# An attention kernel's row norms: channel sums by way of HBM, the root from ScalarE's logarithm and exponential, value transposes two tiles at a time

## The chip, the cores and the metric

The kernel runs on one core of one Trainium2 chip. The metric is device time in microseconds, from the first to the last instruction of the program. Before the change it is 3788.41 us, the median of three runs (3782.36 to 3791.38). All data are float32.

## The reference

The input is x, 48 channels of 256 x 256. Layer 0 is x + attention(groupnorm(x)), and layer 1 is x + window mixing(groupnorm(x)). The change lies in layer 0:

```python
qkv = jnp.einsum('bchw,oc->bohw', x, w_qkv)
qkv = dwconv3x3(qkv, w_dw)
q, k, v = jnp.split(qkv, 3, axis=1)
...
q = _l2norm(q)          # over the channels of a head's token
k = _l2norm(k)
attn = jnp.einsum('bhcn,bhcm->bhnm', q, k) * temperature
attn = jax.nn.softmax(attn, axis=-1)
out = jnp.einsum('bhcn,bhnm->bhcm', v, attn)
```

Between the split and the norm, heads() unfolds 4 x 4 patches: a token is one patch, and a head's token has 6 channels x 16 pixels = 96 entries. There are 8 heads and 4096 tokens inside the image (border tokens are zeros, and enter the softmax's sum as a constant). The norm of a token is the root of the sum of 96 squares: over 16 pixels, and over 6 channels. Queries are also scaled by the temperature, and values aren't scaled at all.

## The kernel before, in words

Everything that the change touches happens in the attention stage, from about 300 to 3320 us. Its outer loop runs over the 8 heads (h), and its inner loop over 16 steps (g) of G = 2 blocks of 128 tokens each. The order of instructions is written out by hand there (tc.manual_schedule): every engine runs its own instructions in the order of the program's text, and waits where its operands or buffers aren't ready.

In step g:

- scores (L536) multiplies a block of 128 queries with all 4096 keys in four PSUM tiles of 1024 columns ("big", three buffers of two banks), six matmuls a tile (logits, L341). ScalarE takes the exponential of each tile (L545) and so frees the tile. Scores of block 2g+1 and of block 2g+2 are made in step g, one step ahead of use.
- normalised (L554) divides the values' tile by the sums of the exponentials on VectorE (L558 to L564): vn.
- weigh (L567) runs for k = 0 to 3. It multiplies the exponentials of both blocks with vn in 64 matmuls (L574) into one "big" tile, and VectorE adds this tile to oacc (L585), which frees it.

So a step takes twelve "big" tiles, in the order weigh 0 to 3 and then eight tiles of logits for the next step; "big" has three buffers, so a tile may be begun when the tile three before it has been read.

Beside this, step g prepares the next head (h+1), one row of patches at a time. The class Depthwise is such a row: 126 partitions, which are 7 bands of the image x 18 channels (6 each of queries, keys and values), and 64 patches. Row r passes through three steps: g = r (n: first), g = r+1 (d: taps, square, reduce, norm, root, scale) and g = r+2 (p: high, low, store). There are ten rows, so d is there for g = 1 to 10. In detail:

- load (SyncE) brings the padded pixels; first (L217, ScalarE) is the first of the nine taps of the 3 x 3 convolution, and tap (L236, VectorE) each of the eight others, 1024 elements a partition.
- square (L247, ScalarE) and reduce (L251, VectorE) give the sum over 16 pixels, ss, 126 x 64.
- norm (L255) adds the six channels on TensorE: a product with "same", a 126 x 126 matrix of ones and zeros, into the PSUM tile pn.
- root (L257) makes the inverse root on VectorE: a first value from integer arithmetic on the bits (L268), three Newton steps of three operations each (L273 to L275), and the affine y * nmul + nadd (L276), which puts the temperature in and leaves values alone.
- scale (L281, VectorE) multiplies the row by it: o, in the order of patches.
- high (L290, ScalarE) rounds o to the format of the fast matmul (oh), low (L294, GpSimd) takes the difference (ol), and store (L299) writes o, oh and ol to the DRAM tile qkv of the head, from GpSimd's queue. Values are read from part 2 (o), queries and keys from parts 0 and 1.

Most row tiles have one buffer (cv pool); sq and ol share one ("t4"), so the next row's square waits until ol has been written out.

load_value (L519) reads 512 tokens of a head's values into vt (two buffers), and turn (L525) transposes such a tile on TensorE into the PSUM tile pst (pool "one", two buffers; pn and the output's transposes live there too); ScalarE copies it out (L530). For the next head, two value tiles are loaded in each of the steps g = 11 to 14, and turned in the same step, one after weigh k = 0 and one after k = 2. Tile m has tokens 512m to 512m + 511; row r of band j holds the tokens 576j + 64r to 576j + 64r + 63.

In head 0, each weigh is also followed by a Strip: the 1 x 1 convolution of two pixel rows for the heads 2 to 7, a product into a "big" tile (L185) which ScalarE reads (L188). With it a step has 16 "big" tiles.

The first head's own rows (depthwise_first) are made before the attention stage; they use norm and root with ScalarE's square root, and the change leaves them as they are.

Of the kernel before, what the change touches and what calls it, by code (L numbers as in the profile page):

```python
# [8 lines left out]
F32 = mybir.dt.float32  # L9
F32R = mybir.dt.float32r  # L10
AF = mybir.ActivationFunctionType
ALU = mybir.AluOpType
# [17 lines left out]
CR = 9  # L30
# [14 lines left out]
def conv_preact_kernel(  # L45
# [28 lines left out]
    t1 = [dram.tile([(h1 - h0) * HC, TR, W + 2], F32, name=f"t1_{h0}") for h0, h1 in GROUPS]  # L74
    qkv = [dram.tile([3, CH, HC * KK, CN + PX], F32, name=f"qkv{h}") for h in range(NH)]

    os_ = dram.tile([NT // TP, C * KK, TP], F32, name="os_")
    x1s = dram.tile([C, H, W], F32, name="x1s")

# [119 lines left out]
    class Depthwise:  # L199
# [53 lines left out]
        def norm(self):  # L253
            self.pn = one.tile([NP1, PX], F32, name="pn", tag="one")
            nc.tensor.matmul(self.pn, lhsT=same, rhs=self.ss, start=True, stop=True)  # L255

        def root(self, on_scalar=False):  # L257
            n = self.pool.tile([NP1, PX], F32, name="n", bufs=2)
            nc.vector.tensor_scalar_max(n, self.pn, 1e-24)
            y = self.pool.tile([NP1, PX], F32, name="y", bufs=2)  # L260
            if on_scalar:
                nc.scalar.activation(n, n, AF.Sqrt)
                nc.vector.reciprocal(y, n)
                nc.vector.tensor_scalar(y, y, nmul[:, self.h : self.h + 1], nadd, ALU.mult, ALU.add)
                self.y = y
                return

            nc.vector.tensor_scalar(  # L268
                y.bitcast(mybir.dt.int32), n.bitcast(mybir.dt.int32), -0.5, 1597463007.0, ALU.mult, ALU.add
            )  # L270
            z = self.pool.tile([NP1, PX], F32, name="z", bufs=self.bufs)
            for _ in range(3):
# [230 lines left out]
    with tc.tile_pool(name="ahead", bufs=2) as ah, tc.tile_pool(name="ae", bufs=3) as ae, tc.tile_pool(  # L503
# [110 lines left out]
        with tc.manual_schedule():  # L614
            load_query(0, 1)
            block = scores(0, 0)
            for h in range(NH):
                more = h + 1 < NH
                rows = {r: Depthwise(h + 1, r) for r in range(CR + 1)} if more else {}
                for g in range(NG):  # L620
# [17 lines left out]
                        load_query(h, g + 2)  # L638
                    elif more:
                        load_query(h + 1, g + 2 - NG)  # L640
                    if p:
                        p.store((2,))
                    if d:
                        for t in range(1, 4):
                            d.tap(t)
# [9 lines left out]

                    if g == 0 and rows:
                        rows[0].load()
                    if p:
                        p.high()
                    if d:  # L660
                        d.square()
                    if n:
                        n.first()
                    for k in range(NK):
                        s = (h * NG + g) * NK + k
                        weigh(h, g, blocks, k)
                        if k == 0 and d:
                            d.reduce()
                        if k == 0 and p:
                            p.low(nc.gpsimd)  # L670
                            p.store((0, 1))
                        for w in strips[s]:
                            w.run(big.tile([128, 2, 512], F32, name="big"))
                        for w in strips[s + 2]:
                            w.load()
                        for w in strips[s - 1] if s else []:
                            w.store()
                        if k == 2 and d:
                            d.norm()
                            d.root()  # L680
                        if k == 2 and g + 1 in rows:
                            rows[g + 1].load()
                        if k == 3 and d:
                            d.scale()
                        if h == 0 and 0 < g <= 6 and k == 0:
                            turn(0, g + 1)
                        if more and CR + 2 <= g < CR + 6 and k in (0, 2):
                            turn(h + 1, (g - CR - 2) * 2 + k // 2)

                        if g == 0 and h > 0 and k == 0:  # L690
                            for m in range(6, 8):
# [248 lines left out]
```

## Time and profile before

| | busy us | share of the span |
|---|---|---|
| TensorE, matmul (PE) | 3511.2 | 93% |
| TensorE, weight load (PEld) | 2913.1 | 77% |
| VectorE (DVE) | 2201.6 | 58% |
| ScalarE (ACT) | 1719.0 | 45% |
| GpSimd (POOL) | 599.8 | 16% |

The span of the profiled run is 3787.3 us. A busy share is a mean over stages: the attention stage has ten steps of a head with depthwise work and six without, and VectorE's load is very different in the two. Rows of the profile name a line (L574), an engine, an operation and the tiles as out<-in. A group's row ends with its busy time and the mean of one instruction in ns, and then the idle time of its engine just before it, with what ended that. In a timeline, the columns are the start in us, the time taken, the engine and the instruction, how many were merged, and in brackets the idle time before. Queues are written as SPq, ACTq and POOLq.

Some rows that the change touches, each as count and mean of one:

| instruction | count | mean ns |
|---|---|---|
| L255 PE matmul into pn | 160 records (two for each of 80 products) | 299 |
| L251 DVE reduce 1024 to 64 | 80 | 1217 |
| L273, L274, L275 DVE, 64 elements | 210 each | 225, 226, 225 |
| L281 DVE scale, 1024 elements | 75 | 1992 |
| L290 ACT high | 80 | 1038 |
| L294 POOL low | 80 | 2368 |
| L299 POOL, issue of a store | 70 to 80 for each of three | 1231 to 1339 |
| L528 PE transposes of values | 256 records | 259 |
| L530 ACT copy of the transposed tile | 64 | 478 |
| ACT table loads | 3 | 1283 |

### The profile page before, as it was taken

The page shows a single profiled execution, that of the slowest core. Times are in us where ns is not written, and L with a number is a line of the kernel's source. Part 1 is how long each engine was busy: PE and PEld are TensorE (multiplying, and loading weights), DVE is VectorE, ACT ScalarE, POOL GpSimd, SP SyncE. Part 2 cuts the span into 40 slices and gives each one's busy share as a digit, 9 for nine tenths or more (in the row PEclk, how much of TensorE's full clock was granted, in tenths as well). Part 3 has the DMA queues.
Part 4 walks back from the last instruction along what each step waited for, and adds up shares of the span by engine and source line. Part 5 has one row for each costly group of instructions (what it writes and reads, how often), then busy time and mean ns, then how long its engine had stood idle before and what let it go on. Part 6 is the DMA issues. An engine that isn't in the chain of part 4 may idle for free.

```text
span 3787.3 us, 99981 instructions
## 1 busy us (share of the span) xinstructions
PE 3511.2 (93%) x44216; PEld 2913.1 (77%) x44216; DVE 2201.6 (58%) x3520; ACT 1719.0 (45%) x2668; POOL 599.8 (16%) x595
## 2 busy tenths in 40 slices
PE   1867999999999999999999999999999999955998
PEld 0225777788888888888888888888888889812776
DVE  5572775169727962895299439934992222266564
ACT  0224665555545554555455445545554444300222
POOL 0030121012301220121122112211220000000011
PEclk9888999999999999999999999999999999966999
DMA  6575666534533542354244424432443100299784
GB/s 138 168 177 153 185 192 172 167 110 118 116 83 99 125 110 75 104 127 106 81 109 117 100 83 117 116 98 76 123 114 93 41 21 19 44 243 188 122 145 90
DMA packets 307459, 441.64 MB, mean 117 GB/s; under 512 B 98298, under 2 KB 232778, under 8 KB 302792
## 3 DMA queue, kind: packets, MB, share of 16 engines
q1 hardware_dynamic: 253590, 270.32, 27.5%
q0 software_dynamic: 48320, 156.61, 18.5%
q10 hardware_dynamic: 5106, 8.21, 1.0%
q8 instruction: 351, 5.75, 0.6%
q14 instruction: 92, 0.75, 0.1%
HBM read 234.76 MB, written 199.95 MB: 115 GB/s over the span
## 4 chain that ended last, share of the span: by engine, by line
PE 82%; DMA 6%; issue 2%; DVE 1%; SPq 1%; ACT 0%; POOL 0%; ACTq 0%; POOLq 0%
PE big L341 36%; PE big L574 35%; PE pb L838 4%; PE pa L816 2%; PE pc L855 2%; PE big L185 1%; DMA pad<-t 1%; DMA x1s<-pxt 1%; PE pt L591 1%; PE pst L528 1%; DMA pxt<-in_x_dram 1%; DMA pot<-os__70 1%; DMA t<-ot 1%; PE pn L255 1%; DMA qkv<-ol 0%
## 5 line engine op out<-in xcount | busy, mean ns | idle before, releaser
L545 ACT ACTIVATE e<-big,nmx 128x1024 f32<-128x1024 f32 x1024 | 1144.3, 1118 | 842.1 <-PE big L341 631.7
L341 PE MATMUL big<-kt,qt 128*128 128x512 f32 x6144 | 1438.5, 393 | 43.9 <-DMA qt<-qkv 29.9
L574 PEld LDWEIGHTS big<-vn,e 128*64 128x64 f32 x32768 | 1367.6, 137 | 86.1 <-ACT e L545 45.1
L574 PE MATMUL big<-vn,e 128*64 128x96 f32 x32768 | 1425.4, 248 | 7.5 <-ACT ot L188 4.1
L341 PEld LDWEIGHTS big<-kt,qt 128*128 128x128 f32 x6144 | 1145.4, 188 | 306.5 <-issue 44.6
L585 DVE TENSOR_TENSOR oacc<-big,oacc 128x768 f32<-128x768 f32 x480 | 458.2, 955 | 706.2 <-PE big L574 706.2
L236 DVE SCALAR_TENSOR_TENSOR acc<-pad,dwt,acc 126x1024 f32<-126x1024 f32 x600 | 777.2, 1296 | 33.6 <-ACT acc L217 17.2
L294 POOL TENSOR_TENSOR ol<-o,oh 126x1024 fp32r<-126x1024 f32 x80 | 189.4, 2368 | 942.2 <-DVE ss L251 804.7
L558 DVE TENSOR_REDUCE zt<-zs 128x1 f32<-128x4 f32 x256 | 39.0, 152 | 361.3 <-ACT e L545 361.3
L545 ACT ACTIVATION_READ_ACCUMULATOR e<-big,nmx 128x1 f32 x1024 | 196.0, 191 | 0.0
L823 DVE TENSOR_TENSOR lzt<-pa,cbias 128x864 f32<-128x864 f32 (+1 forms) x88 | 137.0, 1627 | 99.7 <-PE pa L816 99.7
L845 ACT COPY lyt<-pb 128x512 f32<-128x512 f32 x144 | 84.5, 586 | 215.7 <-PE pb L838 215.7
L299 POOL DMA_DIRECT2D qkv<-o x70 | 86.1, 1231 | 511.0 <-DVE zu L560 243.6
L595 POOL DMA_DIRECT2D os__70<-oo x128 | 65.1, 515 | 594.0 <-ACT oo L593 593.6
L247 ACT ACTIVATE sq<-acc 126x1024 f32<-126x1024 f32 x75 | 79.3, 1058 | 167.8 <-issue 112.2
L281 DVE TENSOR_TENSOR o<-acc,y 126x1024 f32<-126x1024 f32 x75 | 149.4, 1992 | 0.1
L838 PEld LDWEIGHTS pb<-wsb,lzt 128*64 128x64 f32 x2304 | 126.3, 138 | 29.2 <-issue 21.2
L838 PE MATMUL pb<-wsb,lzt 128*64 128x128 f32 x2304 | 142.7, 280 | 2.5 <-issue 2.4
L721 PE MATMUL pps<-pot,wp 96*96 96x512 f32 x128 | 77.9, 776 | 68.3 <-DMA pot<-os__70 68.3
L188 ACT ACTIVATE ot<-big,bias 108x1024 f32<-108x1024 f32 x64 | 71.1, 1112 | 153.9 <-PE big L185 72.0
L217 ACT ACTIVATE acc<-pad,dwt 126x1024 f32<-126x1024 f32 x75 | 85.3, 1137 | 73.3 <-DMA pad<-t 73.3
L721 PEld LDWEIGHTS pps<-pot,wp 96*96 96x96 f32 x128 | 26.6, 215 | 119.1 <-issue 118.6
(115 smaller groups left out, 1888.4 us busy)
## 6 DMA issues: line engine op xcount, KB each, us to landing
pad<-t SPq DMA_DIRECT2D x80, 761.9 KB
qkv<-ol POOLq DMA_DIRECT2D x80, 504.0 KB, 8.9
qkv<-o POOLq DMA_DIRECT2D x70, 504.0 KB, 6.9
qkv<-oh POOLq DMA_DIRECT2D x70, 504.0 KB, 7.4
t<-ot SPq DMA_DIRECT2D x128, 217.7 KB
qt<-qkv SPq DMA_DIRECT2D x176, 96.0 KB
xs<-in_x_dram SPq DMA_DIRECT2D x128, 96.0 KB
os__70<-oo POOLq DMA_DIRECT2D x128, 96.0 KB, 2.2
```

The lines of the kernel that those rows point to most:

```text
L217: nc.scalar.mul(self.acc, self.pad[:, 0:KS, 0:W], dwt[:, self.h, 0:1])
L236: nc.vector.scalar_tensor_tensor(self.acc, self.pad[:, dy : dy + KS, dx : dx + W], dwt[:, self.h, tap : tap + 1], self.acc, ALU.mult, ALU.add,
L281: nc.vector.tensor_tensor(self.o.rearrange("p (a b) x -> p a b x", a=KS), self.acc.rearrange("p a (x b) -> p a b x", b=KS), self.y.rearran ...
L294: eng.tensor_sub(self.ol, self.o, self.oh.bitcast(F32))
L299: eng.dma_start(out=qkv[self.h][i].rearrange("j (c k) n -> (j c) k n", k=KK)[:, :, px], in_=self.o if i == 2 else (self.ol if i else self. ...
L341: nc.tensor.matmul(ps[:, i, :], lhsT=qt[:, r, q0 : q0 + 128], rhs=kts[2 * j + i][:, r // 2, :], start=(r == 0), stop=(r == 2),)
L545: nc.scalar.activation(e[:, j * 1024 : (j + 1) * 1024], ps.rearrange("p a b -> p (a b)"), AF.Exp, bias=nmx[:, b : b + 1], accum_out=zs[:, ...
L574: nc.tensor.matmul(ps[p : p + 64, j // 4, j % 4 * HD : (j % 4 + 1) * HD], lhsT=e[:, mb * 128 + p : mb * 128 + p + 64], rhs=vn, start=(i == 0),
L585: nc.vector.tensor_add(oaccs[h, k], ps[:, :, : 4 * HD], oaccs[h, k])
L721: nc.tensor.matmul(ps[:, i : i + 2, :], lhsT=wp, rhs=ot[:, ki * KS + i : ki * KS + i + 2, :], start=True, stop=True,)
L823: nc.vector.tensor_tensor(zv[:, :, y0 : y0 + n, :], pa[:, :, : n * T3 * C].rearrange("p s (y k) -> p s y k", y=n), cbias.rearrange("p (u v ...
L838: nc.tensor.matmul(pb[s * WS : (s + 1) * WS, i, :], lhsT=zts[u][:, t * C + c + i, :], rhs=wsb[:, t, :], start=True, stop=True,)
```

## The change

The sum over the six channels leaves TensorE. Instead, gather writes ss (32 KB) to a DRAM tile on SyncE's queue, and reads it back so that each of the 126 partitions gets the six rows of its group, sg. One step later guess adds the six on VectorE, bounds the sum from below, and takes ScalarE's logarithm and then the exponential of minus one half of it as a first value of the inverse root. mend refines this with one Newton step on VectorE and applies the affine. For this, root, scale, high, low and all three stores of a row move to step g = r+2: guess stands after weigh k = 0, the rest after k = 1. first of the newest row moves behind them. The turns of the next head's values both stand after weigh k = 0. root itself stays for the branch that isn't taken here and for depthwise_first.

The aim is to free TensorE of the small products and of changes between kinds of matrices, and VectorE of two of three Newton steps.

```diff
+    ssd = [dram.tile([NP1, PX], F32, name=f"ssd{i}") for i in range(2)]
...
+        def gather(self):
+            to = ssd[self.r % 2]
+            nc.sync.dma_start(out=to, in_=self.ss)
+            self.sg = self.pool.tile([NP1, 6, PX], F32, name="sg")
+            nc.sync.dma_start(
+                out=self.sg,
+                in_=to.rearrange("(g u c) n -> g u (c n)", u=1, c=6).to_broadcast([NP1 // 6, 6, 6 * PX]),
+            )
+
+        def guess(self):
+            self.n = n = self.pool.tile([NP1, PX], F32, name="n", bufs=1)
+            nc.vector.tensor_reduce(n, self.sg.rearrange("p c n -> p n c"), AX.X, ALU.add)
+            nc.vector.tensor_scalar_max(n, n, 1e-24)
+            self.y = self.pool.tile([NP1, PX], F32, name="y", bufs=1)
+            nc.scalar.activation(self.y, n, AF.Ln)
+            nc.scalar.activation(self.y, self.y, AF.Exp, scale=-0.5)
+
+        def mend(self):
+            z = self.pool.tile([NP1, PX], F32, name="z", bufs=1)
+            nc.vector.tensor_mul(z, self.y, self.y)
+            nc.vector.scalar_tensor_tensor(z, z, -0.5, self.n, ALU.mult, ALU.mult)
+            nc.vector.scalar_tensor_tensor(self.y, z, 1.5, self.y, ALU.add, ALU.mult)
+            nc.vector.tensor_scalar(self.y, self.y, nmul[:, self.h : self.h + 1], nadd, ALU.mult, ALU.add)
...
-                    if p:
-                        p.store((2,))
...
-                    if p:
-                        p.high()
                     if d:
                         d.square()
-                    if n:
-                        n.first()
                     for k in range(NK):
                         s = (h * NG + g) * NK + k
                         weigh(h, g, blocks, k)
+                        if k == 0 and p:
+                            p.guess()
                         if k == 0 and d:
                             d.reduce()
-                        if k == 0 and p:
+                            d.gather()
+                        if k == 1 and p:
+                            p.mend()
+                            p.scale()
+                            p.high()
                             p.low(nc.gpsimd)
-                            p.store((0, 1))
+                            p.store()
+                        if k == 1 and n:
+                            n.first()
...
-                        if k == 2 and d:
-                            d.norm()
-                            d.root()
...
-                        if k == 3 and d:
-                            d.scale()
...
-                        if more and CR + 2 <= g < CR + 6 and k in (0, 2):
-                            turn(h + 1, (g - CR - 2) * 2 + k // 2)
+                        if more and CR + 2 <= g < CR + 6 and k == 0:
+                            for m in range(2):
+                                turn(h + 1, (g - CR - 2) * 2 + m)
```

More of the change, by code (lines that the diff above doesn't have):

```diff
@@ L255, in norm @@
             nc.tensor.matmul(self.pn, lhsT=same, rhs=self.ss, start=True, stop=True)
+        def gather(self):
[19 more added lines that the diff above has]
+            nc.vector.tensor_scalar(self.y, self.y, nmul[:, self.h : self.h + 1], nadd, ALU.mult, ALU.add)
         def root(self, on_scalar=False):
-            n = self.pool.tile([NP1, PX], F32, name="n", bufs=2)
+            n = self.pool.tile([NP1, PX], F32, name="n", bufs=min(self.bufs, 2))
             nc.vector.tensor_scalar_max(n, self.pn, 1e-24)
-            y = self.pool.tile([NP1, PX], F32, name="y", bufs=2)
+            y = self.pool.tile([NP1, PX], F32, name="y", bufs=min(self.bufs, 2))
             if on_scalar:
```

## The prediction

> **What bounds the kernel now.** I read the chain of work first, then busy times by stretch, then the timeline of one repeated piece, engine by engine.
>
> ```profile
> PE 82%; DMA 6%; issue 2%; DVE 1%; SPq 1%; ACT 0%; POOL 0%; ACTq 0%; POOLq 0%
> PE big L341 36%; PE big L574 35%; PE pb L838 4%; PE pa L816 2%; PE pc L855 2%; PE big L185 1%; DMA pad<-t 1%; DMA x1s<-pxt 1%; PE pt L591 1%; PE pst L528 1%; DMA pxt<-in_x_dram 1%; DMA pot<-os__70 1%; DMA t<-ot 1%; PE pn L255 1%; DMA qkv<-ol 0%
> ```
>
> TensorE's two attention products are 71% of the chain; pn (L255), which the change removes, is on it with 1%. Busy time by stretch (columns: PE, PEld, DVE, ACT, POOL):
>
> ```profile
> 1623.10:1645.40 22.30, 22.30 (x307) 19.85 (x306) 20.74 (x35) 12.69 (x19) 6.02 (x4) 1.00 0.49 120
> 3100.00:3121.80 21.80, 21.80 (x310) 19.51 (x307) 5.24 (x12) 9.65 (x16) 0.00 (x0) 1.00 0.07 20
> 385.60:412.90 27.30, 27.30 (x328) 21.36 (x327) 21.07 (x35) 17.40 (x24) 6.06 (x4) 1.00 0.72 196
> ```
>
> I call a window the time from the first weight load of weigh(k=0) to that of the next g; there are 16 in each head. The rows are a window with depthwise work (head 3), one without (head 7) and one of head 0, where strips run too. PE fills all three; but VectorE has only 1.6 us to spare in the first, so its order may decide who waits. PEld of the first window:
>
> ```profile
> 1623.10 7.95 PEld L574 LDWEIGHTS big<-vn,e 128*64 128x64 f32 x192 [0.35 <-ACT e L545]
> 1631.17 0.29 PEld L255 LDWEIGHTS pn<-ss,same 126*126 126x126 f32 x2
> 1631.53 2.67 PEld L574 LDWEIGHTS big<-vn,e 128*64 128x64 f32 x64
> 1634.32 10.75 PEld L341 LDWEIGHTS big<-kt,qt 128*128 128x128 f32 x48
> 1645.42 0.69 PEld L574 LDWEIGHTS big<-vn,e 128*64 128x64 f32 x16 [0.35 <-ACT e L545]
> ```
>
> The period is 1645.42 - 1623.10 = 22.32 us; without depthwise work it is 3120.14 - 3098.32 = 21.82 in the same view. The difference, 0.50, is pn, 1631.17 to 1631.53, and the changes of weights around it (rather 0.52 over many windows). So PE waits for nobody here, and what goes from PE comes off the time, if nothing new makes it wait.
>
> **What the Trainium skill says.** *ScalarE: Activation LUTs*, section "What ACT_TABLE_LOAD costs": a load takes 1283 ns, with a drain of about 1380 ns 2.66 us per switch. The trace has the 1283; the activation after it starts 1.3 us after the load's start, so no drain follows the load. But ScalarE had been idle, so a drain between busy activations isn't shown:
>
> ```profile
> L534 ACT ACT_TABLE_LOAD x1: 1283/1283/1283, 274.6 to 274.6; - x1
> L534 ACT ACTIVATE e<-nmx x1: 416/416/416, 275.9 to 275.9; 128x256 f32<-128x256 f32 x1
> ```
>
> The same page, "Table sets: the hidden batching unit", knows a set that holds both ln and exp. The changed program's list of ScalarE instructions doesn't use it so: a load stands ahead of each Ln and of each Exp of guess, 140 in 70 rows. *DMA: Bandwidth & Descriptors*, "Anatomy of one DMA — SWDGE (gpsimd) path", puts a transfer's fixed cost at about 2.0 us; the trace agrees, with 2.2 us for the 96 KB of os_.
>
> **The change, part by part.** Three buffers of "big" set the rule: a product may start when the one three before it has been read. In heads 1 to 6 the order is w0 to w3 (weigh), s0 to s7 (logits), so s1 needs w2 read by VectorE (L585).
>
> *1. pn goes.* 60 windows (10 in each of heads 1 to 6) x 0.52 = -31 us, if the period falls to 21.81.
>
> *2. The root moves across three engines.* VectorE loses 12 small operations: 1632.16 to 1635.30, 3.1 us. It gains a reduction of 384 (estimate 0.55: 1024 take 1.22 at L251, plus a fixed part), a maximum (0.2), one Newton step and the affine (3 x 0.26 + 0.32 = 1.1): about 1.9. The relief of 1.2 us is worth nothing by itself, but pulls the taps forward.
>
> ScalarE gains Ln and Exp (0.25 each, as L262) and two loads of 1.28. They lie in the weigh half, where it has room: 12.7 of 22.3 busy. Yet in order: Ln waits for VectorE's maximum, mend on VectorE for Exp, oh (high) for scale, and behind oh are first and the next exps.
>
> VectorE's view of the same window, for the chain:
>
> ```profile
> 1628.76 1.22 DVE L251 TENSOR_REDUCE ss<-sq 126x64 f32<-126x1024 f32 x1 [0.31 <-ACT sq L247]
> 1635.21 0.95 DVE L585 TENSOR_TENSOR oacc<-big,oacc 128x768 f32<-128x768 f32 x1
> 1636.08 1.99 DVE L281 TENSOR_TENSOR o<-acc,y 126x1024 f32<-126x1024 f32 x1
> 1642.58 0.15 DVE L558 TENSOR_REDUCE zt<-zs 128x1 f32<-128x4 f32 x1
> ```
>
> The taps now end 4.49 after the window's start, since zt at 1642.58 is held up by scale and three taps. With scale gone to the middle, zt waits only for the fourth exp (it ends 17.6 into the shorter window): zt 17.7, taps from 18.5, five of 1.31, end 25.05; that is 3.25 in the next. From there: sq to 4.4 (1.06); load 5.7; Ln 5.9; load 7.2; Exp 7.5 (all of VectorE's inputs are ready before: its maximum at 4.8); mend 8.65; scale 10.65; the reading of w2 11.5. PE wants s1 at 10.7 + 1.34 = 12.04. Slack 0.4 us: no wait if a load costs 1.28 to 1.5. With two drains of 1.38 the wait is 2.76 - 0.4 = 2.4 us in every such window. I take the trace's 1.28, and 0.15 us a window for what the slack doesn't cover, since sq also waits for the landing of ol (they share "t4"): ol would be issued at 15.2 and land 24.1, 2.3 into the next window, against 3.3; its slowest landings would miss that. 9 x 6 = 54 windows: +8 us (0 to 25).
>
> *3. Gather.* The 32 KB out and back on SyncE takes two transfers of some 2.2 us; ss is there at 6, sg by 11, needed 15 us later. The pad loads queue behind it and aren't needed before the next window. Nothing, in heads 1 to 6.
>
> *4. Two turns together.* Each block of transposes costs 0.60 now (in a window 11 the weigh loads stop at 1759.73 and go on at 1760.33). Side by side one change of weights is saved: 0.2 (0 to 0.35) x 28 = -6 us. PSUM "one" has a buffer for each.
>
> *5. The stores move later.* The o part left at 15.4 of the window before; now all three leave after low. DMAs now (KB, us to landing):
>
> ```profile
> qkv<-ol POOLq DMA_DIRECT2D x80, 504.0 KB, 8.9
> qkv<-o POOLq DMA_DIRECT2D x70, 504.0 KB, 6.9
> qkv<-oh POOLq DMA_DIRECT2D x70, 504.0 KB, 7.4
> os__70<-oo POOLq DMA_DIRECT2D x128, 96.0 KB, 2.2
> ```
>
> GpSimd: oh there at 11.7, low 2.37 to 14.1, issue of oh to 15.3, ol to 16.5, o from 16.5. It lands 6.9 us later at best, 23.4; queued behind two others (oh and ol land 2.6 us apart now, 7.4 and 1.13 + 8.9 after oh's issue) at 26.7. Who reads row 8? The second value tile: its tokens 512 to 575 are row 8, and the changed program makes that load, issued for g = 11, wait for exactly this store; before, it had landed almost a window earlier. So the load starts 1.6 to 4.9 into window 11, takes 0.8 of issue and 2.2 to 3.1 (192 KB of kt by GpSimd land in 3.1), and is there at 4.6 to 8.8. The second turn, now at k = 0, would run at 3.2; it was at k = 2 and is in PE's queue ahead of w1. PE waits 1.4 to 5.6, say 3.6, in six heads: +22 us.
>
> *6. Head 0.* Here a strip's product follows each weigh, and ScalarE must empty it. ScalarE's window of before:
>
> ```profile
> 386.82 1.04 ACT L290 CAST oh<-o 126x1024 fp32r<-126x1024 f32 x1
> 388.88 1.06 ACT L247 ACTIVATE sq<-acc 126x1024 f32<-126x1024 f32 x1 [1.02 <-DVE acc L236]
> 389.85 1.13 ACT L217 ACTIVATE acc<-pad,dwt 126x1024 f32<-126x1024 f32 x1
> 390.89 1.10 ACT L188 ACTIVATE ot<-big,bias 108x1024 f32<-108x1024 f32 x1
> 393.95 1.11 ACT L188 ACTIVATE ot<-big,bias 108x1024 f32<-108x1024 f32 x1 [1.59 <-issue]
> ```
>
> The second ot ends at 9.45, and w3 needs its buffer. In the changed order it stands behind oh and first, and oh behind scale. w1 ends at 7.0, so its reading ends at 8.2, mend 9.25, scale 11.25, oh 12.35, first 13.4, second ot 14.4. w3 can start at 14.5; it started at 397.95, or 12.34. So +2.1 us in windows 2 to 10, pn's removal included: 9 x 2.1 = +19, and +1 for window 11, with one row still to scale. (The first ot, after Exp, ends at 8.5 and holds w2 up by 0.4, which this wait swallows.) Together +20 (5 to 35: the strips' input loads also queue behind gather).
>
> *Sum:* -31 + 8 - 6 + 22 + 20 = +13 us: 3788 + 13 = 3801.
>
> **The rivals.**
> *A, faster.* The store and its reader overlap better, and head 0's strips find room. For it: PE is the bound, and 0.52 a window is sure to go. Against: the order of ScalarE's queue in head 0, and that the load names the store. -31 - 6 + 8 + 5 = -24: 3764.
> *B, ScalarE's switches become the bound.* The full 2.66. For it: the page; against: the L534 line. 54 x 2.4 + 9 x 2.76 = +155 beside +5 of the rest (the 8 are in it): 3948.
> *C, they cancel.* Smaller waits at row 8 (1.4 x 6 = 8) and head 0 (15) with all else: -31 + 8 - 6 + 8 + 15 = -6, so 3782.
>
> **How the numbers follow.** My forecast 0.46, A 0.22, B 0.12, C 0.20. Slower is the forecast and B, 0.58; same is C. The range must hold 8 in 10: downward from A's upper half, 3768; upward by +25 for part 2 and the upper ends of 5 and 6 in part, 3852. About half of A and B lie outside.
>
> **What would show it.** L255 only 10 rows, 20 records; periods of 21.8 to 22.0 in windows 2 to 10 of heads 1 to 6 (24.2 for B); 140 more loads of 1283 ns, with Ln right behind; PE waiting for a DMA of vt at L528 in six windows; PE waiting for ot (L188) before w3 in head 0, period near 29.4. Wrong it would be if windows of heads 1 to 6 stay above 22.3, or window 11 shows no wait for vt.

## The result, and the profile after

The changed kernel takes 3870.95 us (median of 6 runs, 3862.63 to 3880.75) against 3782.45 for the kernel before (6 runs, 3776.57 to 3791.38). The ratio is 1.0246, with a 95% interval of 1.023 to 1.0262: it is slower, as forecast, but by 88 us where 13 were forecast, and above the 3852 at which the forecast's range ends. The profiled spans are 3878.9 and 3787.3 us. The chain of work that ended last, first by engine and then by line:

```profile
PE 47%; DVE 22%; DMA 12%; ACT 5%; issue 4%; POOL 1%; SPq 1%; ACTq 0%; DVEq 0%; POOLq 0%
PE big L369 19%; PE big L602 18%; DVE acc L237 12%; PE pb L864 4%; DVE o L309 3%; DMA qkv<-ol 3%; DMA pxt<-in_x_dram 2%; DVE oacc L613 2%; DVE zu L588 2%; PE pa L842 2%; DMA qkv<-o 2%; ACT L274 2%; PE pc L881 2%; ACT sq L248 2%; DMA vt<-qkv 1%
```

The two attention products fell from 71% of the chain to 37%; taps, scale and zu on VectorE, and the stores of ol and o, took their place. VectorE's busy share is 58% before and after, but its work now stands in the chain that others wait for. (Lines have moved: weigh L574 is L602, logits L341 is L369, oacc L585 is L613, zu L560 is L588, low L294 is L322.)

With a window as the prediction defines it, the two profiled runs differ as follows (us, 91.6 in all):

| windows | before | after | difference |
|---|---|---|---|
| head 0, all 16 | 458.46 | 492.83 | +34.37 |
| heads 1 to 6, g = 1 | 133.96 | 130.88 | -3.08 |
| g = 2 to 10 (54 windows) | 1205.64 | 1225.53 | +19.89 |
| g = 11 (6) | 139.61 | 182.65 | +43.04 |
| g = 12 to 14 (18) | 415.80 | 410.04 | -5.76 |
| the rest (g = 0 and 15, head 7, start, end) | | | +3.1 |

Now the same views as in the prediction. Busy time by stretch (PE, PEld, DVE, ACT, POOL, then the granted clock, the DMA share and GB/s): a window with depthwise work, and the stretch behind a wait in window 11.

```profile
1679.60:1702.30 22.70, 22.14 (x307) 19.48 (x306) 21.59 (x29) 15.46 (x23) 6.09 (x4) 1.00 0.53 132
...
1828.90:1835.80 6.90, 6.90 (x133) 6.83 (x134) 2.34 (x6) 0.48 (x1) 0.00 (x0) 0.79 0.39 99
```

TensorE no longer fills the first: 22.14 of 22.70. Its weight loads in that window (head 3, g = 5):

```profile
1679.59 10.59 PEld L602 LDWEIGHTS big<-vn,e 128*64 128x64 f32 x256 [0.35 <-ACT e L573]
1690.30 1.23 PEld L369 LDWEIGHTS big<-kt,qt 128*128 128x128 f32 x6
1692.51 9.40 PEld L369 LDWEIGHTS big<-kt,qt 128*128 128x128 f32 x42 [0.98 <-DVE oacc L613]
```

pn is gone from between the weigh loads, and a wait of 0.98 us for oacc stands after the first logits tile: it is s1 waiting for the reading of w2. VectorE there:

```profile
1678.84 5.25 DVE L237 SCALAR_TENSOR_TENSOR acc<-pad,dwt,acc 126x1024 f32<-126x1024 f32 x4
...
1688.40 0.23 DVE L280 TENSOR_TENSOR z<-y 126x64 f32<-126x64 f32 x1 [0.46 <-ACT y L275]
...
1689.59 2.01 DVE L309 TENSOR_TENSOR o<-acc,y 126x1024 f32<-126x1024 f32 x1
1691.51 1.81 DVE L613 TENSOR_TENSOR oacc<-big,oacc 128x768 f32<-128x768 f32 x2
1693.24 0.15 DVE L586 TENSOR_REDUCE zt<-zs 128x1 f32<-128x4 f32 x1
1693.42 1.76 DVE L588 SCALAR_TENSOR_TENSOR zu<-e,zt 128x1 f32<-128x1 f32 x1
...
1695.41 0.96 DVE L592 TENSOR_SCALAR vn<-vT,rz 128x96 f32<-128x96 f32 x1
1695.60 3.92 DVE L237 SCALAR_TENSOR_TENSOR acc<-pad,dwt,acc 126x1024 f32<-126x1024 f32 x3
...
1699.62 0.16 DVE L588 SCALAR_TENSOR_TENSOR zu<-e,zt 128x1 f32<-128x1 f32 x1
```

The zu of one block took 1.76 us, that of the next 0.16, on operands of the same shape. The long one ended at 1695.18. GpSimd there:

```profile
1692.76 2.40 POOL L322 TENSOR_TENSOR ol<-o,oh 126x1024 fp32r<-126x1024 f32 x1 [16.59 <-ACT oh L318]
1695.11 1.23 POOL L327 DMA_DIRECT2D qkv<-oh  x1
1696.25 1.35 POOL L327 DMA_DIRECT2D qkv<-ol  x1
1697.37 1.47 POOL L327 DMA_DIRECT2D qkv<-o  x1
```

low ended at 1695.16. In all, 60 of the 256 zu take 1.75 to 1.78 us, one in each window of heads 1 to 6 in which low runs. vn, 0.27 for the next block, took 0.96 while the first issue ran, but the taps behind it still began 0.19 after it, as they do behind a short one. Before, low ran from 6.96 to 9.32 of a window, beside the readings of weigh tiles in PSUM, and zu was short (low, then VectorE):

```profile
1630.06 2.36 POOL L294 TENSOR_TENSOR ol<-o,oh 126x1024 fp32r<-126x1024 f32 x1 [12.68 <-DVE ss L251]
```

```profile
1631.29 0.96 DVE L585 TENSOR_TENSOR oacc<-big,oacc 128x768 f32<-128x768 f32 x1 [0.45 <-PE big L574]
...
1638.16 0.16 DVE L560 SCALAR_TENSOR_TENSOR zu<-e,zt 128x1 f32<-128x1 f32 x1
```

ScalarE of the changed kernel in the window of g = 5:

```profile
1684.18 1.06 ACT L248 ACTIVATE sq<-acc 126x1024 f32<-126x1024 f32 x1 [3.27 <-DVE acc L237]
1685.25 1.28 ACT L274 ACT_TABLE_LOAD   x1
1686.55 0.26 ACT L274 ACTIVATE y<-n 126x64 f32<-126x64 f32 x1
1686.82 1.28 ACT L275 ACT_TABLE_LOAD   x1
1688.11 0.26 ACT L275 ACTIVATE y<-y 126x64 f32<-126x64 f32 x1
```

There is the switch between busy activations that the trace of before lacked: 1.28 us, the Ln 0.02 us later, no drain. Now window 11 of head 3, TensorE and then SyncE's queue:

```profile
1817.76 2.67 PEld L602 LDWEIGHTS big<-vn,e 128*64 128x64 f32 x64 [0.35 <-ACT e L573]
1820.55 0.37 PEld L556 LDWEIGHTS pst<-ident,vt 96*128 96x128 f32 x4
1828.14 0.61 PEld L556 LDWEIGHTS pst<-ident,vt 96*128 96x128 f32 x4 [7.22 <-issue]
1828.97 1.26 PEld L602 LDWEIGHTS big<-vn,e 128*64 128x64 f32 x16 [0.22 <-issue]
```

```profile
1804.65 0.81 SPq L263 DMA_DIRECT2D sg<-ssd  x1
1805.78 20.25 SPq L343 DMA_DIRECT2D vt<-qkv  x3
```

The second turn waits 7.22 us for its value tile: the loads of vt stand in SyncE's queue for 20 us. After it, 16 weight loads take 1.26 us, 0.079 each, where 64 took 2.67, 0.042 each: the clock is halved. The stores that vt waits for (KB, median us to landing):

```profile
qkv<-ol POOLq DMA_DIRECT2D x80, 504.0 KB, 9.8
qkv<-oh POOLq DMA_DIRECT2D x70, 504.0 KB, 7.7
qkv<-o POOLq DMA_DIRECT2D x70, 504.0 KB, 10.9
```

The o part landed 6.9 us after issue before, and 10.9 now that it goes last.

### The profile page after: what moved, and what is told of

Its sections match the earlier page's. It is cut to its first block, busy times and chain, and to the rows that moved or that the text cites. A ratio compares the mean times of both kernels' runs of the same rounds, so it can differ in the third digit from the quotient of the medians.

```text
span 3878.9 us, 99718 instructions
## 1 busy us (share of the span) xinstructions
PE 3509.3 (90%) x44076; PEld 2907.2 (75%) x44076; DVE 2248.0 (58%) x3100; ACT 1918.0 (49%) x2948; POOL 602.7 (16%) x595
## 4 chain that ended last, share of the span: by engine, by line
PE 47%; DVE 22%; DMA 12%; ACT 5%; issue 4%; POOL 1%; SPq 1%; ACTq 0%; DVEq 0%; POOLq 0%
PE big L369 19%; PE big L602 18%; DVE acc L237 12%; PE pb L864 4%; DVE o L309 3%; DMA qkv<-ol 3%; DMA pxt<-in_x_dram 2%; DVE oacc L613 2%; DVE zu L588 2%; PE pa L842 2%; DMA qkv<-o 2%; ACT L274 2%; PE pc L881 2%; ACT sq L248 2%; DMA vt<-qkv 1%
## 5 line engine op out<-in xcount | busy, mean ns | idle before, releaser
L369 PE MATMUL big<-kt,qt 128*128 128x512 f32 x6144 | 1456.2, 395 | 76.6 <-DVE oacc L613 31.1
L602 PEld LDWEIGHTS big<-vn,e 128*64 128x64 f32 x32768 | 1381.2, 139 | 94.6 <-ACT e L573 45.1
L602 PE MATMUL big<-vn,e 128*64 128x96 f32 x32768 | 1423.6, 249 | 9.2 <-ACT ot L189 4.9
L369 PEld LDWEIGHTS big<-kt,qt 128*128 128x128 f32 x6144 | 1143.8, 189 | 358.0 <-DVE oacc L613 51.2
L613 DVE TENSOR_TENSOR oacc<-big,oacc 128x768 f32<-128x768 f32 x480 | 453.0, 954 | 745.7 <-PE big L602 745.6
L322 POOL TENSOR_TENSOR ol<-o,oh 126x1024 fp32r<-126x1024 f32 x80 | 191.6, 2395 | 1661.3 <-ACT oh L318 1661.3
L318 ACT CAST oh<-o 126x1024 fp32r<-126x1024 f32 x80 | 83.7, 1047 | 285.6 <-DVE o L309 285.6
L864 PEld LDWEIGHTS pb<-wsb,lzt 128*64 128x64 f32 x2304 | 126.3, 138 | 29.2 <-issue 19.9
L588 DVE SCALAR_TENSOR_TENSOR zu<-e,zt 128x1 f32<-128x1 f32 x256 | 134.3, 525 | 8.8
L592 DVE TENSOR_SCALAR vn<-vT,rz 128x96 f32<-128x96 f32 x256 | 113.5, 444 | 9.7 <-DMA qt<-qkv 0.7
## 6 DMA issues: line engine op xcount, KB each, us to landing
qkv<-o POOLq DMA_DIRECT2D x70, 504.0 KB, 10.9
```

The source lines that it names most:

```text
L322: eng.tensor_sub(self.ol, self.o, self.oh.bitcast(F32))
L369: nc.tensor.matmul(ps[:, i, :], lhsT=qt[:, r, q0 : q0 + 128], rhs=kts[2 * j + i][:, r // 2, :], start=(r == 0), stop=(r == 2),)
L588: nc.vector.scalar_tensor_tensor(zu, e0[:, b : b + 1], float(NBORDER), zt, ALU.mult, ALU.add)
L592: nc.vector.tensor_scalar_mul(vn, values[h, nb // 4][:, nb % 4, :], rz)
L602: nc.tensor.matmul(ps[p : p + 64, j // 4, j % 4 * HD : (j % 4 + 1) * HD], lhsT=e[:, mb * 128 + p : mb * 128 + p + 64], rhs=vn, start=(i == 0),
L613: nc.vector.tensor_add(oaccs[h, k], ps[:, :, : 4 * HD], oaccs[h, k])
```

## The experiments

"Expected" is the text on record. The theory after reading the traces was that low, moved onto the time of VectorE's zu, holds the chain up; the rivals were the table switches, the store of row 8, and SyncE's queue. Differences by windows are against the kernel before, in one profiled run each, and are sums over the windows named. A ratio is to the kernel before as it ran beside the experiment; its medians lie between 3771.5 and 3782.5 us, so experiments are better compared by their ratios than by their times.

**The switches taken out of the chain** (Ln replaced by Identity, which needs no other table):

```diff
-            nc.scalar.activation(self.y, n, AF.Ln)
+            nc.scalar.activation(self.y, n, AF.Identity)
```

> The logarithm in guess is replaced by a plain copy (Identity), so every ScalarE function is in one table set and no load is needed; the first value of the root, and with it the output, is no inverse root any more, and this run is for its time alone. Theory M (late store of row 8, VectorE held up in the middle of the window, head 0's order): the chain gets shorter by two loads, 2.57 us, but mend then waits for the reading of w1, so scale comes only about 0.5 us earlier; windows 4 to 10 of heads 1 to 6 go from 22.7 to 22.2 and window 11 stays near 30; about 3845 us. Rival S (the table switches are the cost): most of the 89 us come back, under 3800 us.

Measured: 3827.8 us, ratio 1.0153 (1.012 to 1.0186). The windows g = 4 to 10 have a median of 22.15 us, where the changed kernel has 22.69 and the kernel before 22.33: two loads in the chain cost 0.54 a window, as expected, and don't bring it to 21.81. Over g = 2 to 10 that is -12.4 instead of +19.9. Window 11 stays at +44.4; head 0 falls to +18.9, which nobody expected, and so the total lies below the 3845 forecast. zu is still held (1.75 to 1.78 us), and the taps still end 4.5 into the window. In 13 of the 54 windows the square comes later still (in one at 4.96, with the taps done at 4.51): there the landing of ol ("t4") is last.

**The row's o stored before high and low:**

```diff
                             p.scale()
+                            p.store((2,))
                             p.high()
                             p.low(nc.gpsimd)
-                            p.store()
+                            p.store((0, 1))
```

> All work is done, only the order on GpSimd differs: o is stored right after scale, before low and the two other stores. Theory M: row 8's o lands near 20 us of window 10, so the second value tile is there in time, window 11 of heads 1 to 6 falls from 30.4 to about 23, no halved clock follows, and the time falls by some 43 us to 3828. Rival S: window 11's wait came from ScalarE's loads ahead of the copies of the transposed tiles; then nothing changes, 3870.

Measured: 3865.5 us, ratio 1.0235 (1.0209 to 1.0262). The wait of window 11 went as expected (+1.4 us over six windows instead of +43), but the total didn't follow. GpSimd issues o ahead of low; in window 5 of head 3 low starts at 14.16 and zu takes 2.26 us (14.43 to 16.69), and the windows g = 2 to 10 go to a median of 23.15 (+41.5 in all), head 0 to +48.3. That the late store of o makes window 11 wait is confirmed. With low 0.9 us later, zu is held longer (2.14 us at least), and the gain is lost elsewhere.

**low in four pieces,** so that what waits for it waits for a quarter:

```diff
-            eng.tensor_sub(self.ol, self.o, self.oh.bitcast(F32))
+            for i in range(0, KK, 4):
+                q = slice(i, i + 4)
+                eng.tensor_sub(self.ol[:, q], self.o[:, q], self.oh[:, q].bitcast(F32))
```

> low is done in four instructions of 256 elements instead of one of 1024. Theory M: zu on VectorE (1.76 us in these windows, 0.16 else) waits for GpSimd's running instruction to end; with pieces it waits under 0.7 us, the taps end about 1 us sooner, and the windows fall from 22.7 to about 22.0: some 35 us off, 3836. Rival: zu is late for another reason (its own operands); then it stays at 1.76 and the time at 3870.

Measured: 3906.9 us, ratio 1.0363 (1.033 to 1.0395): a miss. GpSimd and, in the next fence, VectorE (head 3, g = 5):

```profile
1691.03 3.82 POOL L324 TENSOR_TENSOR ol<-o,oh 126x256 fp32r<-126x256 f32 x4 [16.12 <-ACT oh L318]
```

```profile
1691.69 0.16 DVE L590 SCALAR_TENSOR_TENSOR zu<-e,zt 128x1 f32<-128x1 f32 x1
...
1692.45 4.79 DVE L237 SCALAR_TENSOR_TENSOR acc<-pad,dwt,acc 126x1024 f32<-126x1024 f32 x3
```

zu is back at 0.16 in all 54 windows, as the theory has it: what waits, waits for one piece at most. But the pieces take 3.82 us instead of 2.40 (0.74 each for three, and 1.72 for the last, beside the taps), and the taps behind zu are slowed: three take 4.79, where 3.92 is their time undisturbed. The taps still end earlier, at a median of 3.92 instead of 4.49, but ol lands later, and in 42 of 54 windows the next square waits for it (in window 5 of head 3 it began at 5.55 though the taps had ended at 3.95). The median of g = 4 to 10 is 23.19, so here one long instruction was cheaper than four short ones.

**Gather's two transfers on GpSimd's queue:**

```diff
-            nc.sync.dma_start(out=to, in_=self.ss)
+            nc.gpsimd.dma_start(out=to, in_=self.ss)
...
-            nc.sync.dma_start(
+            nc.gpsimd.dma_start(
                 out=self.sg,
```

> Both transfers of gather are issued by GpSimd instead of SyncE. Theory M: in head 0 the loads of strips and values no longer queue behind gather's two waits, and the waits of TensorE for vt and xs there (10 to 15 us with the halved clock after them) shrink: 10 to 20 us off, all in head 0, 3850 to 3860; heads 1 to 6 as before. Rival: head 0 is slow by ScalarE's order alone (the strip's reading behind scale and high); then under 5 us off.

Measured: 3858.1 us, ratio 1.0216 (1.0181 to 1.0252). Head 0 falls from +34.4 to +7.9, by more than the 10 to 20 expected; window 11 stays (+42.1). The issues push low some 0.3 us later, and g = 2 to 10 go from +19.9 to +29.4.

**The kernel before with paired turns alone:**

```diff
-                        if more and CR + 2 <= g < CR + 6 and k in (0, 2):
-                            turn(h + 1, (g - CR - 2) * 2 + k // 2)
+                        if more and CR + 2 <= g < CR + 6 and k == 0:
+                            for m in range(2):
+                                turn(h + 1, (g - CR - 2) * 2 + m)
```

> The kernel before with one part of the change alone, the two turns side by side after weigh k = 0. Theory M: windows 11 to 14 lose 0.32 us each, as windows 12 to 14 did in the changed kernel, and the o part is stored as early as before, so nothing waits: 28 x 0.32 = 9 us off, 0.9976 of the time before. Rival: the second turn waits for its tile in window 11 even with the early store; then no gain or slower.

Measured: 3770.8 us beside 3777.9, ratio 0.9981 (0.9971 to 0.999), 7 us faster where 9 were expected. Windows 12 to 14 give -5.76, exactly what they give in the changed kernel, and in five heads window 11 gives its -0.32 too: with o stored early, its reader doesn't wait even at k = 0. The sixth, that of head 6, takes 3.8 more; TensorE waits there 3.2 us between two tiles of logits, far from the turns, and why stays open.

**low left out** (oh is stored a second time in place of ol):

```diff
-                    in_=self.o if i == 2 else (self.ol if i else self.oh).bitcast(F32),
+                    in_=self.o if i == 2 else (self.ol if i and hasattr(self, 'ol') else self.oh).bitcast(F32),
...
-                            p.low(nc.gpsimd)
```

> The changed kernel with low left out: the rounding remainder of queries and keys isn't computed, and oh is stored a second time in its place, so the logits are less exact; all transfers stay. Theory M (GpSimd's low holds VectorE up, and late ol holds the next sq up): zu falls from 1.76 to 0.16 us, windows 4 to 10 of heads 1 to 6 from 22.7 to 21.8 to 22.0, that is 40 to 48 us off; the stores start 2.4 us sooner, so window 11 shrinks by about 2 us too (12 to 15 us); about 3812. Rival: the chain through ScalarE's table loads alone sets the window; then zu is short and the windows stay at 22.7.

Measured: 3834.0 us, ratio 1.0143 (1.0114 to 1.0171), expected 3812. All of the windows g = 2 to 10 run at 21.81 (-27.7 in all), and the taps end at 3.24. The rows of zu over the whole run (ns: least, median, most), first of the changed kernel, then without low:

```profile
L588 DVE SCALAR_TENSOR_TENSOR zu<-e,zt x256: 158/159/1776, 317.4 to 3383.8; 128x1 f32<-128x1 f32 x128
```

```profile
L588 DVE SCALAR_TENSOR_TENSOR zu<-e,zt x256: 158/159/163, 312.3 to 3338.2; 128x1 f32<-128x1 f32 x128
```

TensorE, without low (head 3):

```profile
1687.59 10.75 PEld L369 LDWEIGHTS big<-kt,qt 128*128 128x128 f32 x48
```

48 loads of logits without a gap, and both table switches are still there, so the switches alone don't set the period of heads 1 to 6. Without low, though, no square waits for the landing of ol either, so this run alone doesn't part the two; the last two reorderings, which keep low and its store, do. The total missed because head 0 went to +62.5, with 71.7 us at the halved clock (window 11 came down to +24.1); why head 0 suffers more without low stays open.

**The changed kernel with its turns apart again** (k = 0 and 2):

```diff
-                        if more and CR + 2 <= g < CR + 6 and k == 0:
-                            for m in range(2):
-                                turn(h + 1, (g - CR - 2) * 2 + m)
+                        if more and CR + 2 <= g < CR + 6 and k in (0, 2):
+                            turn(h + 1, (g - CR - 2) * 2 + k // 2)
```

> The changed kernel with the two turns of the next head's values apart again, after weigh k = 0 and k = 2. Theory M: the value tile still lands some 10 us into window 11, but PE wants it only at 8.7, so window 11 falls from 30.4 to about 25, no halved clock follows; windows 12 to 14 give back 0.32 each: some 27 us off, 3844. Rival: if something other than the tile's landing held PE there, window 11 stays near 30.

Measured: 3842.3 us, ratio 1.0168 (1.014 to 1.0197). Window 11 costs +5.7 instead of +43.0: the late store hurts through the early second turn. Windows 12 to 14 are those of the kernel before (23.10 each), but for one of head 6 that takes 6.0 more, with a wait of 4.2 us for an exponential, cause open.

**A version after these findings.** high, low and the stores of oh and ol go back to the window after (q, a fourth row), o is stored right after scale, gather is cut in two, send and fetch, so that no queue stands for it, and both turns follow k = 2. In short:

```diff
+                    if q: q.high()                    # ahead of weigh k = 0
...
+   k == 0: d.reduce(); q.low(nc.gpsimd); q.store((0, 1)); p.guess()
+   k == 1: d.send()                                  # ss to HBM
+   k == 2: p.mend(); p.scale(); p.store((2,)); both turns
+   k == 3: n.first(); d.fetch()                      # sg from HBM
```

> All parts of the change, put elsewhere: guess after the strip of k = 0, mend and scale after weigh k = 2, o stored right then, high, low and the other two stores one step later, where they were before the change; gather's two transfers issued after k = 1 and k = 3; first after k = 3; both turns after k = 2. Theory M: no product of TensorE waits, windows 1 to 10 are 21.8 to 22.0 in heads 1 to 6 and window 11 under 23; head 0 within 5 us of before: 25 to 45 us off the time before, 0.988 to 0.993. Rival S (the switches between table sets cost it): 140 switches are still there, so it stays slower than before.

Measured: 3801.8 us, ratio 1.0055 (1.0037 to 1.0073): a miss. Window 11 is at -2.9 and head 0 at +11.8, but g = 2 to 10 have a median of 22.82 (+20.2). VectorE, and then GpSimd, in one of these windows:

```profile
1645.68 0.82 DVE L272 TENSOR_REDUCE n<-sg 126x64 f32<-126x384 f32 x1
1646.54 1.73 DVE L273 TENSOR_SCALAR n<-n 126x64 f32<-126x64 f32 x1
```

```profile
1645.85 2.37 POOL L323 TENSOR_TENSOR ol<-o,oh 126x1024 fp32r<-126x1024 f32 x1 [13.60 <-DVE ss L252]
```

Now the maximum of guess is caught: 1.73 us instead of 0.20, up to low's end at 1648.22. The reduction ahead of it, beside low for most of its time, isn't held. So the theory met a second trial that nobody had planned.

**The same, with guess's VectorE part ahead of reduce** (so ahead of low); Ln and Exp stay behind, as raw. First with gather on SyncE, then on GpSimd:

```diff
+        def raw(self):
...
+                        if k == 0 and p:
+                            p.guess()
                         if k == 0 and d:
                             d.reduce()
...
-                            p.guess()
+                            p.raw()
```

> The reordered kernel with one thing moved: guess's two VectorE operations stand before reduce, and its logarithm and exponential still behind the strip. In the first reordering, the maximum came after reduce, just when GpSimd's low ran, and took 1.73 instead of 0.20 us. Theory M: the maximum is short again, windows 4 to 10 of heads 1 to 6 go from 22.8 to 21.8 to 22.0; 55 to 65 us less than the first reordering's heads 1 to 6 give some 3750, 0.990 to 0.994 of the time before. Rival: the windows are held by ScalarE's chain and stay at 22.5 or more.

> As the run before it, with gather's two transfers issued by GpSimd. Theory M: head 0 gets rid of the waits for xs that gather's extra transfers on SyncE make (5 to 15 us), heads 1 to 6 stay at 21.8 to 22.2: 0.987 to 0.992 of the time before. Rival: the transfers' issue on GpSimd holds VectorE up in mend and scale; then the windows of heads 1 to 6 are longer than in the run before.

Measured: 3747.3 us, ratio 0.9911 (0.9891 to 0.9931), and 3738.2 us, ratio 0.9892 (0.9872 to 0.9912), beside 3779.9 for the kernel before. Both beat both kernels, by about 1% the one before. In both, g = 2 to 10 give -27.7, g = 1 -3.1 and window 11 -2.9; windows 12 to 14 give -4.8 and -1.4 (window 12 of head 6 is longer there than the others, by 0.9 and 4.3); head 0 gives +2.6 with gather on SyncE and -6.9 on GpSimd. From the second, VectorE's maximum and its neighbours, and then low on GpSimd:

```profile
1650.91 0.83 DVE L272 TENSOR_REDUCE n<-sg 126x64 f32<-126x384 f32 x1
1651.78 0.20 DVE L273 TENSOR_SCALAR n<-n 126x64 f32<-126x64 f32 x1
...
1653.02 0.95 DVE L616 TENSOR_TENSOR oacc<-big,oacc 128x768 f32<-128x768 f32 x1
```

```profile
1653.18 2.37 POOL L325 TENSOR_TENSOR ol<-o,oh 126x1024 fp32r<-126x1024 f32 x1 [6.96 <-DVE ss L252]
```

low runs beside oacc, which reads PSUM and keeps its 0.95.

**Single costs added to the kernel before.** Gather's two transfers as extra work on SyncE, behind reduce (root's tiles n and y get one buffer each here, as in the changed kernel):

```diff
                             d.reduce()
+                            d.gather()
```

> The kernel before, with gather's two transfers added as extra work on SyncE after reduce; nobody reads sg, and norm and root stay. Theory M: SyncE stands still for about 4 us behind reduce in every row, which only head 0 feels (its loads of strips and values): 15 to 30 us slower, all in head 0. Rival (head 0 of the changed kernel is slow by ScalarE's order): within 5 us of before.

Measured: 3850.4 us, ratio 1.0187 (1.0161 to 1.0214), some 70 us where 15 to 30 were expected. Heads 1 to 6 don't change; head 0 takes +75.8, with 78.5 us more at the halved clock. SyncE's queue in head 0:

```profile
456.19 8.98 SPq L325 DMA_DIRECT2D qt<-qkv  x12
467.13 0.32 SPq L260 DMA_DIRECT2D ssd<-ss  x1
468.57 0.81 SPq L262 DMA_DIRECT2D sg<-ssd  x1
469.42 1.71 SPq L180 DMA_DIRECT2D xs<-in_x_dram  x2
```

From 465.17 the queue issues nothing until ss is there, and nothing between 467.45 and 468.57, until the write has landed. The strip's inputs (xs) stand behind it: in head 0 TensorE waits 56.8 us ahead of the strips' products, and 5.2 in the kernel before.

Two switches a row as extra work on ScalarE (an Ln and an Exp on ones, nobody waits for the result):

```diff
                         d.square()
+                        d.switch()
```

> The kernel before, with the two table switches of guess added for each row as extra work (a logarithm and an exponential of ones, after square; nobody reads them). It prices the switches where nothing waits for their result. Theory M: each costs 1.28 us of ScalarE, which has room in heads 1 to 6, so nothing there; in head 0 the first strip's reading comes 3 us later and holds the third weigh up: 5 to 15 us slower in all. Rival S: 140 switches of 2.66 us, on the path: over 60 us slower.

Measured: 3806.2 us, ratio 1.0063 (1.0041 to 1.0085), some 26 us where 5 to 15 were expected. All of it is in head 0 (+24.7); the windows of heads 1 to 6 stay at 22.33. In head 0 TensorE waits 42.5 us for the strips' readings (ot), 10.5 in the kernel before. So 120 switches there cost nothing beside the chain, while in it two cost 0.54 a window (first experiment).

## Why the prediction was right or wrong

**Part 1, pn: right.** Windows of g = 1, where pn went and little else changed, fell by 0.51; all of g = 2 to 10 reach 21.81 once nothing holds the chain (low left out, and the last two reorderings). The -31 are there: -27.7 and -3.1 in the best version.

**Part 2, the chain: here it failed**, at the step "zt waits only for the fourth exp", and so at "taps from 18.5, five of 1.31, end 25.05; that is 3.25 in the next". They ended 4.49 in. The prediction placed low at 11.7 to 14.1 on GpSimd, as if GpSimd's work touched nobody. How it goes wrong can be seen in window 2 of a head, the first with a guess, which has no low in the window ahead of it. There the taps end 3.24 in, and the window takes 21.81, both as forecast. But low runs in it, from 12.0 on, and holds zu for 1.6 us (head 3, the window from 1612.41):

```profile
1611.72 3.93 DVE L237 SCALAR_TENSOR_TENSOR acc<-pad,dwt,acc 126x1024 f32<-126x1024 f32 x3
...
1625.06 1.78 DVE L588 SCALAR_TENSOR_TENSOR zu<-e,zt 128x1 f32<-128x1 f32 x1
...
1631.10 0.15 DVE L586 TENSOR_REDUCE zt<-zs 128x1 f32<-128x4 f32 x1
...
1631.86 6.56 DVE L237 SCALAR_TENSOR_TENSOR acc<-pad,dwt,acc 126x1024 f32<-126x1024 f32 x5
```

So the three taps between the two zt end late, the second zt comes at 18.7 instead of 17.7, and the five taps end 4.2 into window 3. From window 4 on the chain has closed to a ring, from the taps over square, Ln, Exp, scale and zu to the next taps, and its length sets the window. Behind the taps the working held: from their end to Exp's end it had 4.25 us (measured 4.49 to 8.77, 4.28), mend 1.15 (1.12), scale 2.0 (2.0). Being 1.24 late, less the slack of 0.4, is 0.84 of the 0.88 by which the mean window (22.69) stands above 21.81; the sum had 0.15. As 54 windows that is +48 instead of +8, and it turns -28 into +20. Without low the second zt comes at 17.72, the taps start at 18.49 and end at 3.24: the forecast's chain. That low's run is the cause is shown by this, by the pieces, and most cleanly by the maximum, which was held beside low and is short once it stands ahead of it, with low and its store in place.

A second term of part 2 was too small as well: ol landed 3.7 into the next window (median; 2.6 to 5.6) instead of 2.3, since low began at 13.2 instead of 11.7 and the landing took 9.8 instead of 8.9. In 12 of the 54 windows the square waited for it, up to 1.2 us beyond the taps.

The Trainium skill has this, in *SBUF — State Buffer*, section "Who interferes with whom": VectorE and GpSimd share one pair of ports to SBUF; a VectorE instruction with both inputs in SBUF contends with a GpSimd instruction that reads SBUF, a tensor_scalar can enter a mode that takes the pair, the first to start keeps it for its whole instruction, and reductions don't contend. The runs agree in each: zu 1.76 instead of 0.16, the maximum 1.73 instead of 0.20, oacc (one input from PSUM) at 0.95 beside low, the reduction 0.82 beside it and 0.83 without. That the shared pair is what does it is the page's account; the runs show who is held, and until when. The prediction didn't bring it to bear; in the window shown of the kernel before, low met only readings of PSUM. What stretches vn during an issue, and why only in some windows, stays open; in the windows shown it delayed nobody.

**Rival B, the full 2.66 a switch: wrong**, as its evidence against had it. The Ln starts 0.02 us after its load, itself 0.01 after the square, and two loads in the chain were worth 0.54 a window. Where the figure of 2.66 in *ScalarE: Activation LUTs*, "What ACT_TABLE_LOAD costs", and this trace differ, the trace decides. Rivals A and C needed small waits at row 8 and in head 0, and fall with parts 5 and 6; only the last two reorderings reached what A hoped for.

**Part 3, gather: right for heads 1 to 6** (gather alone leaves their windows unchanged), but in head 0 it is the largest cost; see part 6. The way back is 189 KB and not 32, since each partition gets six rows.

**Part 4, turns: right in kind**, -0.32 a window instead of -0.2; -5.8 in windows 12 to 14, where it had 6 for all 28.

**Part 5, row 8's store: the mechanism right, two terms too small.** "Queued behind two others at 26.7" was 28 to 30: low started later, and o took 9.5 to 12.5 us from issue. So the six waits were 4.39 to 7.22 us, mean 5.7, instead of 3.6. The second term wasn't in the sum: after each such wait TensorE runs at half clock for a while, 6.83 us of it in each window 11, partly within the wait, none in the kernel before. *TensorE: Matmul & The Clock Gate*, section "What's actually happening", puts the half clock after at least one idle window of about 3.4 us; these waits are all longer. But the runs set it lower: in heads 1 to 7 of all fourteen traces, each of the 37 waits of 2.7 us or more, with TensorE neither loading nor multiplying, brought 3.4 us or more of half clock, four of 2.1 to 2.5 did and others of up to 2.5 didn't, and none under 2.0 did. The measurement decides. With +7.2 a window, 5.7 of it wait, it comes to +43 instead of +22. Storing o first took it away, moving the turns back most of it.

**Part 6, head 0: the size too small (+34 instead of +20), and the main mechanism missed.** The step "w3 can start at 14.5", waiting for the second ot, isn't what held it. TensorE in a window of head 0, changed kernel:

```profile
425.55 2.67 PEld L602 LDWEIGHTS big<-vn,e 128*64 128x64 f32 x64 [0.78 <-ACT ot L189]
429.84 0.42 PEld L186 LDWEIGHTS big<-xs,wr 48*108 48x108 f32 x4 [1.62 <-DVE oacc L613]
```

w3 did start 14.25 into the window, near the forecast, but that was luck: the long wait ahead of it ended with VectorE's reading of a weigh tile, and with gather on GpSimd w3 started at 12.50 (g = 7 to 9) while the second ot ended only at 14.01. Such a window takes 27.4 us, 0.6 more than before instead of 2.1. What counted most was named in a bracket, "the strips' input loads also queue behind gather": SyncE's queue stands twice for each row, xs and vt come late, and the clock halves (44.4 us of half clock in head 0, 17.1 before). Gather on GpSimd took 26 of the 34 back. ScalarE's order has a share all the same: TensorE's waits for ot grew from 10.5 to 21.7 us, and head 0 fell by 15 with the switches out. The parts don't add: gather alone costs head 0 76 us, the switches alone 25, the whole change 34.

**The sum.** -31 + 8 - 6 + 22 + 20 = +13 as forecast; as measured -31 + 48 - 6 + 43 + 34 = +88, and 3 of start and end make the 91 by which the profiled runs differ. That it came out slower was forecast by parts 5 and 6, which were large and of the right sign; part 2, priced at 8, turned out the largest, through a wait that isn't in it.

## What to carry to other kernels

Before moving a GpSimd instruction, list what VectorE does in the place where it will run: here operations that read PSUM and reductions went on beside it, two with their inputs in SBUF stood still until it ended, and a 0.16-us operation in a chain then cost ten times its length. A store and its reader should be costed from landing, with the queue ahead of it, and a wait of TensorE of more than some 2 us with the halved clock that may follow. A transfer that waits for a computed value doesn't belong in a queue that also carries the loads of others.

## What the runs showed of the hardware

- zu, a VectorE operation on 128 x 1 elements, took 1.75 to 1.78 us instead of 0.16 beside a GpSimd subtraction that reads SBUF (2.26 with o stored first); the maximum, 126 x 64, took 1.73 instead of 0.20. One that reads PSUM kept its 0.95, and a reduction its 0.82.
- The same subtraction in four pieces took 3.82 us instead of 2.40, and the taps beside it took 4.79 instead of 3.92.
- ScalarE's table loads between busy activations take 1.28 us and nothing more: 120 of them beside the chain cost heads 1 to 6 nothing.
- Three stores of 504 KB one behind the other in GpSimd's queue landed 7.7, 9.8 and 10.9 us after issue; the third took 6.9 while it was issued alone and early.
- Waits of 4.4 to 7.2 us each brought 6.8 us of halved clock; over all runs the shortest wait that brought any took 2.1 us, and every one from 2.7 us on did.
- Two small transfers a row, in a queue that stood for their values, cost 76 us in a stage of 458; the time at half clock in it grew by 78.5 us.
